# Scan decays in PSUM and 32-channel scan units in a decoder layer kernel (state space block, cross attention, ternary feed-forward)

## Chip, cores and metric

The kernel runs on one core of one Trainium2 chip. The metric is the device time of one execution in microseconds (us), the median of several runs. The engines are named as in the profile: PE is TensorE (matmuls; PEld its weight loads), DVE is VectorE, ACT is ScalarE, POOL is GpSimd, SP is SyncE, which issues all the DMAs of this kernel.

## What is computed

A batch of 16 sequences, 256 positions of width 512, goes through three blocks, each followed by x = layernorm(x + block(x)), all in float32.

```python
# 1. state space block: 1024 channels d, 16 states n, 256 steps l
hs, gate = x @ W_in_states.T, x @ W_in_gates.T
hs = silu(conv4(hs) + conv_b)                       # causal, along l
dt = softplus((hs @ W_dt.T) @ W_dtproj.T + b_dtproj)
Bm, Cm = hs @ W_b.T, hs @ W_c.T                     # 16 states each
dA  = exp(-exp(A_log) * dt)                         # decay, [d, n, l]
dBu = dt * Bm * hs                                  # input, [d, n, l]
h_l = dA_l * h_{l-1} + dBu_l                        # the scan along l
y = sum_n(h * Cm) + D * hs
out = (y * silu(gate)) @ W_out.T
# 2. cross attention: 16 heads of 16, 512 x 512 scores a head,
#    softmax(mask * q.k / 4 - (1 - mask) * 1e6) * mask, times v
# 3. feed-forward: activations rounded to 8 bits, ternary weights,
#    silu(a) * b, rounded again, down projection
```

## The kernel before

The function decoder_kernel writes the work of each batch as short pieces (Python functions) in named streams: G and P are the projections (prep), R the step widths dt and the rows B and C, M the scan, T and U the output projection, K, L, A and N the attention, F the feed-forward. The table WIN gives each stream a stretch of time, counted in batches from the start of its batch's scan; place spreads the pieces over it, and the pieces of all batches are emitted in the order of these times. So the scan of one batch, the attention of the one before and the feed-forward of the one before that run side by side. The framework's scheduler then fixes the order of instructions on each engine; each engine works its list in order.

**Scan (lines 351 to 403).** Channels are on partitions, 128 in each of eight tiles d. A unit is one tile d and four of the 16 states, 4 x 256 columns. POOL makes the scan's input (line 382, B times dt*u); ACT makes the decay with four exponentials, one a state, with a different scale each (line 392), into one of two SBUF buffers dA; VectorE scans 1024 columns in one instruction (line 394), where a zero first decay of each state stops the carry from the state before. Three units later (LAG) POOL multiplies by C (line 362), in six of eight units VectorE adds the upper two states to the lower two (line 369), and PE adds up the states by matmuls with an identity into the PSUM tile red (line 371). At the end of a tile d VectorE adds D*u (line 374). B and C are DMA-broadcast to all 128 partitions.

```python
t = dA_t[dA_i[0] % DAB]
for j in range(4):
    n = q * 4 + j
    nc.scalar.activation(t[:, j, 1:], st["dt"][d // 4][:, d % 4, 1:], AF.Exp, scale=A[:, d, n : n + 1])
nc.vector.tensor_tensor_scan(seg, t.rearrange("p n l -> p (n l)"), seg, 0.0, ALU.mult, ALU.add)
```

**Projections (240 to 348).** inproj makes u with three convolution steps on VectorE (line 280), a tanh and a product of two SBUF tensors (line 287). gate computes silu(gate) early (lines 253 to 264), stores it in DRAM (sgd), and gated (line 466) loads it back when the scan is done. softplus works on SBUF tiles of 1024 columns (lines 333 to 348), and dtu is formed in the scan (line 379).

**Attention (406 to 593).** split_store (line 434) writes q and k to DRAM in a part of reduced precision and a remainder (line 440). step(i) computes the scores of a head twice: once for the row maxima (lines 505 and 535), and once transposed, where ACT takes the exponentials (line 540), which are multiplied by the values with 32 columns of weights (line 546). Each of four heads has its own quarter of PE's columns (tile_position); the product of a head comes after that head's exponentials.

**PSUM.** Its eight banks are shared out by BANK (line 40): two for projections, output and feed-forward (mm), four for scores and attention projections (sc), one for the values' sums (av), one for the states' sums (red). The norm (line 223) and the feed-forward's scale factors (lines 600 to 613) mix tiny VectorE steps with one POOL power (line 231).

Of the kernel before, what the change touches and what calls it, by code (L numbers as in the profile page):

```python
# [36 lines left out]
WIN = {'G': (-1.4, -1.15), 'P': (-1.15, -0.888), 'R': (-0.611, -0.455), 'M': (0.0, 0.8), 'T': (0.476, 0.576), 'U': (0.812, 0.912), 'L': (0.991, 1.041), 'K': (0.773, 0.826), 'A': (1.018, 1.938), 'N': (2.099, 2.147), 'F': (2.57, 3.237), 'W': (0.0, 1.0)}  # L37
DAB = 2
UB = 4
BANK = {k: ("mm", 2) for k in "PGOFDW"} | {k: ("sc", 4) for k in "VXKQS"} | {"Y": ("av", 1), "E": ("red", 1)}  # L40
VW = HD + 1
HB = 5
PTB = 5
QKB = 10
SPT, SPN = "h", HB
F4B = 3
ONPOOL = "n"
LAG = 3
SGB = 1
S2OFF = 2  # L50
TREE_V = (0,1,3,4,5,7)
# [3 lines left out]
def decoder_kernel(ctx, tc, x, xT, ctx_in, mask, winT, wdtT, wbcT, wdpT, woutT, dvec, wqkvT, bqk, bv, wguT, wdnT, out):  # L55
# [15 lines left out]
    def eng(k):  # L71
        return nc.gpsimd if k in ONPOOL else nc.vector

# [32 lines left out]
    # A = -exp(A_log); conv weights and D, W_c carry the halves of the tanh forms  # L106
    A = const([P, NDT, NS], F32, "A")
    nc.scalar.activation(A, dv[:, :, 7:23], AF.Exp)
    nc.vector.tensor_scalar(A, A, -1.0, None, ALU.mult)
# [8 lines left out]

    dA_t = []
    for i in range(DAB):  # L120
        t = const([P, 4, L], F32, f"dA{i}")
        nc.vector.memset(t[:, :, 0:1], 0.0)
        dA_t.append(t)
    dA_i = [0]

# [5 lines left out]
    # Score operands in DRAM, 64 rows a head: rows 2..49 three slots of split q or k, 50..55 split  # L131
    # mask terms, 0, 1, 62, 63 ones in k and zeros in q (the maxima take their place on chip).
# [90 lines left out]
    def layernorm(r, o):  # L223
        st = at("lst", [P, 2, 6], 2)
        mv = at("lmv", [P, 2, 2], 2)
        for i in range(2):
            nc.vector.bn_stats(st[:, i, :], r[:, i, :])
            nc.vector.bn_aggr(mv[:, i, :], st[:, i, :])
        rs = at("lrs", [P, 2], 2)
        nc.vector.tensor_scalar(rs, mv[:, :, 1], LN_EPS, None, ALU.add)  # L230
        nc.gpsimd.tensor_tensor(rs, rs, mhalf, ALU.pow)  # L231
        nb = at("lnb", [P, 2], 2)
        nc.vector.scalar_tensor_tensor(nb, mv[:, :, 0], -1.0, rs, ALU.mult, ALU.mult)
        for i in range(2):
            nc.scalar.activation(o[:, i, :], r[:, i, :], AF.Identity, bias=nb[:, i : i + 1], scale=rs[:, i : i + 1])
# [4 lines left out]
    def prep(b):  # L240
# [3 lines left out]
        def load():  # L244
            st["xT"] = []
            for k in range(4):
                t = mt("xT", [P, L], 4)
                nc.sync.dma_start(out=t, in_=xT[b, k * P : (k + 1) * P, :])
                st["xT"].append(t)
            st["u"] = [None, None]  # L250
            st["sgd"] = dr.tile([P, NDT, L], F32, tag="sgd", name=nm("sgd"), bufs=3)

        def gate(d0):
            g = mm_ps([P, 2, L], "G")
            for i in range(2):
                d = d0 + i
                w = mt("win", [P, 4, P], 3)
                nc.sync.dma_start(out=w, in_=winT[:, :, DI + d * P : DI + (d + 1) * P])
                for k in range(4):
                    nc.tensor.matmul(g[:, i, :], w[:, k, :], st["xT"][k], start=k == 0, stop=k == 3)  # L260
            sg = mt("sg", [P, 2, L], SGB)
            nc.scalar.activation(sg, g, AF.Tanh, scale=0.5)
            nc.vector.scalar_tensor_tensor(sg, sg, 1.0, g, ALU.add, ALU.mult)  # L263
            nc.sync.dma_start(out=st["sgd"][:, d0 : d0 + 2, :], in_=sg)

        def inproj(d0):
            hs = mm_ps([P, 2, L], "P")
            z = mt("tmp", [P, 2, L], 2)
            for i in range(2):
                d = d0 + i  # L270
                w = mt("win", [P, 4, P], 3)
                nc.sync.dma_start(out=w, in_=winT[:, :, d * P : (d + 1) * P])
                for k in range(4):
                    nc.tensor.matmul(hs[:, i, :], w[:, k, :], st["xT"][k], start=k == 0, stop=k == 3)  # L274
# [11 lines left out]
            nc.scalar.activation(u, z, AF.Tanh)  # L286
            eng("z").scalar_tensor_tensor(u, u, 1.0, z, ALU.add, ALU.mult)  # L287
# [20 lines left out]
        def bcast():  # L308
            st["B"], st["C"] = [], []
            for half in range(2):  # L310
                for nmk, o in (("B", 0), ("C", NS)):
                    t = mt(nmk, [P, 8, L], 2)
                    src = st["bcd"][o + half * 8 : o + half * 8 + 8, :]
                    nc.sync.dma_start(out=t, in_=src[None].broadcast_to([P, 8, L]))
                    st[nmk].append(t)

        def dtpre():
            st["dt"] = []
            for hf in range(2):
                X = mt("dt", [P, 4, L], 3)  # L320
                st["dt"].append(X)
# [9 lines left out]

        def softplus():
            xs = [X.rearrange("p a l -> p (a l)") for X in st["dt"]]
            es = []
            for X in xs:
                e = mt(SPT, [P, 4 * L], SPN)
# [3 lines left out]
            for X, e in zip(xs, es):  # L340
                W = mt(SPT, [P, 4 * L], SPN)
                nc.vector.tensor_scalar(W, e, 1.0, -1.0, ALU.add, ALU.add)
                eng("r").scalar_tensor_tensor(X, X, 0.0, W, ALU.max, ALU.subtract)
                eng("x").tensor_tensor(X, X, e, ALU.add)
            for e in es:
                nc.scalar.activation(e, e, AF.Ln, bias=1.0)
            for X, e in zip(xs, es):
                nc.vector.tensor_tensor(X, X, e, ALU.add)  # L348

        g = [load] + [lambda d=d: gate(d) for d in range(0, NDT, 2)]  # L350
        th = [lambda d=d: inproj(d) for d in range(0, NDT, 2)]
        return {"G": g, "P": th, "R": [ts_bc, bcast, dtpre, softplus]}

# [1 line left out]
    def scan(b):  # L355
        st = S[b]
        th = []
        pend = []

        def tail(job):  # L360
            d, q, hh = job
            nc.gpsimd.tensor_tensor(hh, hh, st["C"][q // 2][:, 4 * (q % 2) : 4 * (q % 2) + 4, :], ALU.mult)  # L362
            if q == 0:
                st["red"] = mm_ps([P, 512], "E")
            red = st["red"]
            m = 4
            if (4 * d + q) % 8 in TREE_V:
                m = 2
                nc.vector.tensor_tensor(hh[:, 0:2, :], hh[:, 0:2, :], hh[:, 2:4, :], ALU.add)  # L369
            for n in range(m):  # L370
                nc.tensor.matmul(red[:, :L], ident, hh[:, n, :], start=q + n == 0, stop=q == 3 and n == m - 1)  # L371
            if q == 3:
                u = st["u"][d // 4][:, d % 4, :]
                nc.vector.scalar_tensor_tensor(u, u, dv[:, d, 5:6], red[:, :L], ALU.mult, ALU.add)

        def unit(d, q):
            if q == 0:
                dtu = mt("dtu", [P, L], 2)
                nc.vector.tensor_tensor(dtu, st["dt"][d // 4][:, d % 4, :], st["u"][d // 4][:, d % 4, :], ALU.mult)  # L379
                st["dtu"] = dtu  # L380
            hh = mt("h", [P, 4, L], HB)
            nc.gpsimd.tensor_tensor(  # L382
                hh,
                st["B"][q // 2][:, 4 * (q % 2) : 4 * (q % 2) + 4, :],
                st["dtu"][:, None, :].broadcast_to([P, 4, L]),
                ALU.mult,
            )
            t = dA_t[dA_i[0] % DAB]
            dA_i[0] += 1
            for j in range(4):  # L390
                n = q * 4 + j
                nc.scalar.activation(t[:, j, 1:], st["dt"][d // 4][:, d % 4, 1:], AF.Exp, scale=A[:, d, n : n + 1])  # L392
            seg = hh.rearrange("p n l -> p (n l)")
            nc.vector.tensor_tensor_scan(seg, t.rearrange("p n l -> p (n l)"), seg, 0.0, ALU.mult, ALU.add)  # L394
            pend.append((d, q, hh))
# [3 lines left out]
        for d in range(NDT):  # L399
            for q in range(4):  # L400
                th.append(lambda d=d, q=q: unit(d, q))
# [4 lines left out]
    def attn(b):  # L406
# [4 lines left out]
        def load():  # L411
# [14 lines left out]
            st["so"] = dr.tile([4, P, H], F32, tag="so", name=nm("so"), bufs=2)  # L426
# [348 lines left out]
```

## Time and profile before

| | |
|---|---|
| three runs | 5077.5, 5086.9, 5097.3 us; median 5086.9 us |
| profiled execution, span from first to last instruction | 5091.4 us |
| granted PE clock, mean | 0.874 of full |
| DMA | 592.7 MB on the main queue, 37.1% of 16 engines' time |
| ACT exponentials of the decay (line 392) | 2048 x 496 ns |
| row maxima (line 535) | 1024 x 678 ns |
| ACT waits for the scan before it fills dA | 1127.2 us, 403 times |

In a row of instructions the profile gives the line, the engine, the operation, out<-in by tile name, the shape and the count; then after the bar the busy time in us, the mean duration in ns, and the engine's idle time just before these instructions with what ended it. A row of one tile's instructions gives shortest, median and longest duration in ns. The chain of work that ended last runs for 50% of its time over DVE and for 29% over PE.

### The profile page before, as it was taken

To read this page: it belongs to the slowest core of one execution; us is meant where nothing else is said; L and a number is where in the kernel's file an instruction comes from. 1 tells how busy PE (TensorE), PEld (TensorE's weight loads), DVE (VectorE), ACT (ScalarE), POOL (GpSimd) and SP (SyncE) were. 2 spreads that over 40 slices of the span, in tenths; PEclk is the share of its full clock that TensorE was granted. 3 is DMA by queue.
4 is the path that set the end of the run, shared out by engine and by line. 5 is a ranking of instruction groups with operands and counts; after the bars stand their busy time and mean duration, and the time that the engine had idled before them with its cause. 6 is when DMAs were issued, how large, how long until landed. Compare 5 with 4: busy or idle time off the path is not lost.

```text
span 5091.4 us, 41958 instructions
## 1 busy us (share of the span) xinstructions
PE 4207.6 (83%) x12802; PEld 1966.2 (39%) x12802; DVE 4421.5 (87%) x4282; ACT 2284.0 (45%) x4506; POOL 3229.4 (63%) x1143
## 2 busy tenths in 40 slices
PE   6456877988889898888888899897888889887986
PEld 4333343444433444444344344343444334333332
DVE  4999899989999898999989897997979899898542
ACT  3243434444445444444544444454454444443433
POOL 2747767858678485767757584685849577477100
PEclk8677888988889898889989889898999989897988
DMA  7362232343432434344243433424343243333332
GB/s 210 106 216 88 77 115 81 119 125 115 124 129 80 134 113 132 120 121 134 88 143 100 130 115 114 135 85 130 112 140 114 78 151 97 116 106 96 96 109 79
DMA packets 416618, 595.42 MB, mean 117 GB/s; under 512 B 47416, under 2 KB 203064, under 8 KB 408200
## 3 DMA queue, kind: packets, MB, share of 16 engines
q1 hardware_dynamic: 416392, 592.74, 37.1%
q8 instruction: 101, 1.65, 0.1%
q14 instruction: 125, 1.02, 0.1%
HBM read 493.39 MB, written 105.51 MB: 118 GB/s over the span
## 4 chain that ended last, share of the span: by engine, by line
DVE 50%; PE 29%; issue 7%; DMA 5%; ACT 2%; POOL 1%; SPq 1%; DVEq 0%; ACTq 0%; POOLq 0%
DVE h L394 19%; PE av L546 8%; DVE h L369 7%; DVE mx L535 6%; PE sc L505 6%; PE red L371 4%; DVE dtu L379 2%; PE mm L481 2%; DVE tmp L280 2%; PE mm L260 1%; PE mm L677 1%; PE mm L274 1%; DVE u L287 1%; DVE qf L440 1%; DVE dt L348 1%
## 5 line engine op out<-in xcount | busy, mean ns | idle before, releaser
L382 POOL TENSOR_TENSOR h<-B,dtu 128x1024 f32<-128x1024 f32 x512 | 1622.3, 3178 | 511.7 <-PE red L371 182.3
L362 POOL TENSOR_TENSOR h<-h,C 128x1024 f32<-128x1024 f32 x512 | 1480.0, 2896 | 652.3 <-DVE h L394 607.2
L394 DVE TENSOR_TENSOR_SCAN h<-dA,h 128x1024 f32<-128x1024 f32 x512 | 1614.5, 3157 | 2.3 <-POOL h L382 2.2
L392 ACT ACTIVATE dA<-dt,A 128x255 f32<-128x255 f32 x2048 | 877.3, 496 | 1192.3 <-DVE h L394 1127.2
L546 PE MATMUL av<-pT,vaug 128*32 128x512 f32 x2048 | 1039.0, 646 | 10.8 <-ACT pT L540 10.3
L371 PE MATMUL red<-h,ident 128*128 128x256 f32 x2560 | 770.6, 439 | 318.9 <-DVE h L369 271.3
L505 PE MATMUL sc<-qk,qk 64*128 64x512 f32 x2048 | 865.1, 518 | 195.6 <-DVE mx L535 103.9
L535 DVE TENSOR_REDUCE mx<-sc 128x1 f32<-128x512 f32 x1024 | 672.4, 678 | 264.2 <-PE sc L505 262.6
L540 ACT ACTIVATE pT<-sc 128x512 f32<-128x512 f32 x1024 | 581.7, 588 | 474.5 <-PE sc L505 472.9
L505 PEld LDWEIGHTS sc<-qk,qk 64*128 64x128 f32 x2048 | 351.1, 203 | 1101.7 <-issue 670.0
L371 PEld LDWEIGHTS red<-h,ident 128*128 128x128 f32 x2560 | 520.8, 215 | 557.6 <-DVE h L369 334.4
L369 DVE TENSOR_TENSOR h<-h 128x512 f32<-128x512 f32 x384 | 663.8, 1730 | 1.6 <-POOL h L362 1.6
L481 PE MATMUL mm<-wout,u 128*128 128x512 f32 x512 | 297.8, 692 | 40.1 <-DMA wout<-in_woutT 17.6
L581 POOL TENSOR_TENSOR qk<-qk,qk 128x512 f32<-128x512 f32 x32 | 47.9, 1498 | 443.9 <-DMA qk<-sr 340.7
L274 PE MATMUL mm<-xT,win 128*128 128x256 f32 x1024 | 273.7, 417 | 37.9 <-DMA win<-in_winT 21.3
L260 PE MATMUL mm<-xT,win 128*128 128x256 f32 x1024 | 264.7, 412 | 44.1 <-DMA win<-in_winT 20.9
L546 PEld LDWEIGHTS av<-pT,vaug 128*32 128x32 f32 x2048 | 132.3, 111 | 324.3 <-issue 223.1
L260 PEld LDWEIGHTS mm<-xT,win 128*128 128x128 f32 x1024 | 204.3, 206 | 120.1 <-DVE f L639 32.7
L274 PEld LDWEIGHTS mm<-xT,win 128*128 128x128 f32 x1024 | 205.0, 207 | 105.4 <-issue 28.7
L280 DVE SCALAR_TENSOR_TENSOR tmp<-mm,cw,tmp 128x254 f32<-128x254 f32 (+2 forms) x384 | 180.0, 471 | 36.9 <-ACT tmp L277 33.4
L231 POOL TENSOR_TENSOR lrs<-lrs,mhalf 128x2 f32<-128x2 f32 x48 | 53.4, 1118 | 246.4 <-DVE lrs L230 237.3
L642 PE MATMUL mm<-fw,xqT 128*128 128x512 fp8e4 x512 | 153.9, 429 | 38.5 <-DVE sg L263 18.4
(116 smaller groups left out, 3927.7 us busy)
## 6 DMA issues: line engine op xcount, KB each, us to landing
win<-in_winT SPq DMA_DIRECT2D x256, 256.0 KB
wout<-in_woutT SPq DMA_DIRECT2D x256, 256.0 KB
fw<-gu_q SPq DMA_DIRECT2D x256, 256.0 KB
B<-bcd SPq DMA_DIRECT2D x32, 1024.0 KB
C<-bcd SPq DMA_DIRECT2D x32, 1024.0 KB
qk<-sq SPq DMA_DIRECT2D x128, 256.0 KB
qk<-sk SPq DMA_DIRECT2D x128, 256.0 KB
fw<-dn_q SPq DMA_DIRECT2D x128, 256.0 KB
```

The source lines that it names most:

```text
L260: nc.tensor.matmul(g[:, i, :], w[:, k, :], st["xT"][k], start=k == 0, stop=k == 3)
L274: nc.tensor.matmul(hs[:, i, :], w[:, k, :], st["xT"][k], start=k == 0, stop=k == 3)
L362: nc.gpsimd.tensor_tensor(hh, hh, st["C"][q // 2][:, 4 * (q % 2) : 4 * (q % 2) + 4, :], ALU.mult)
L369: nc.vector.tensor_tensor(hh[:, 0:2, :], hh[:, 0:2, :], hh[:, 2:4, :], ALU.add)
L371: nc.tensor.matmul(red[:, :L], ident, hh[:, n, :], start=q + n == 0, stop=q == 3 and n == m - 1)
L382: nc.gpsimd.tensor_tensor(hh, st["B"][q // 2][:, 4 * (q % 2) : 4 * (q % 2) + 4, :], st["dtu"][:, None, :].broadcast_to([P, 4, L]), ALU.mult,)
L392: nc.scalar.activation(t[:, j, 1:], st["dt"][d // 4][:, d % 4, 1:], AF.Exp, scale=A[:, d, n : n + 1])
L394: nc.vector.tensor_tensor_scan(seg, t.rearrange("p n l -> p (n l)"), seg, 0.0, ALU.mult, ALU.add)
L505: nc.tensor.matmul(p, lhs[rows, c * P : (c + 1) * P].bitcast(F32R), rhs[rows, :].bitcast(F32R), start=True, stop=True)
L535: nc.vector.tensor_reduce(st[("mx", i // G)][:, i % G, k : k + 1], p, AX.X, ALU.max)
L540: nc.scalar.activation(e, p, AF.Exp, scale=DSC)
L546: nc.tensor.matmul(av[32 * k : 32 * k + 32, :], vaug_f[:, i2 % 4, c0 : c0 + 32], pT[k], start=i2 % 4 == 0, stop=i2 % 4 == 3, tile_position ...
```

## The change

It touches many places at once. A scan unit becomes 32 channels and all 16 states: four groups of states on the partitions (4 x 32), four states and 256 steps on the columns. For this dt and dt*u go through DRAM (dtd) and are loaded replicated (dtr, dur), and B and C are loaded once per group of states. The decay is written to two PSUM banks, two states each, and each unit has two scans of 512 columns. The adds of line 369 are gone; the states' sums of four units are taken together by matmuls with 32 columns of weights (sel) in four column groups. The values' products also come in four groups of 256 columns, all after the exponentials of two heads. The gate is projected where it is used and not stored. VectorE steps that had two SBUF operands take one of them from PSUM (u, softplus, q/k remainder, gate). Tiny steps of norm and feed-forward go to POOL. PSUM: two banks mm (projections, output, states' sums), three sc (scores, attention projections, feed-forward), two dA, one av. The h buffers grow from five to eight; pT becomes three buffers of two heads.

```diff
-BANK = {k: ("mm", 2) for k in "PGOFDW"} | {k: ("sc", 4) for k in "VXKQS"} | {"Y": ("av", 1), "E": ("red", 1)}
+BANK = {k: ("mm", 2) for k in "PGOE"} | {k: ("sc", 3) for k in "VXKQSFDW"}
-HB = 5
-PTB = 5
+NB4 = 4
+DB = P // NB4
+HB = 8
+PTB = 3
-LAG = 3
+LAG = 2
...
+    sel = const([P, DB], F32, "sel")
+    nc.vector.tensor_reduce(sel, ident.rearrange("p (n d) -> p d n", n=NB4), AX.X, ALU.add)
...
-    for i in range(DAB):
-        t = const([P, 4, L], F32, f"dA{i}")
+    for i in range(2):
+        t = ps.tile([P, 2, L], F32, tag=f"dA{i}", name=f"dA{i}", bufs=1)
...
-        nc.vector.tensor_scalar(rs, mv[:, :, 1], LN_EPS, None, ALU.add)
+        nc.gpsimd.tensor_scalar(rs, mv[:, :, 1], LN_EPS, None, ALU.add)
         nc.gpsimd.tensor_tensor(rs, rs, mhalf, ALU.pow)
-        nc.vector.scalar_tensor_tensor(nb, mv[:, :, 0], -1.0, rs, ALU.mult, ALU.mult)
+        nc.gpsimd.tensor_tensor(nb, mv[:, :, 0], rs, ALU.mult)
+        nc.gpsimd.tensor_scalar(nb, nb, -1.0, None, ALU.mult)
...
-            nc.scalar.activation(u, z, AF.Tanh)
-            eng("z").scalar_tensor_tensor(u, u, 1.0, z, ALU.add, ALU.mult)
+            nc.scalar.activation(hs, z, AF.Tanh)
+            nc.vector.scalar_tensor_tensor(u, hs, 1.0, z, ALU.add, ALU.mult)
...
+                    t = mm_ps([P, 2, L], "P")
+                    nc.scalar.activation(t, e, AF.Identity, bias=1.0)
+                    nc.vector.scalar_tensor_tensor(t, t, 1.0, e, ALU.subtract, ALU.subtract)
+                    nc.vector.scalar_tensor_tensor(t, X, 0.0, t, ALU.max, ALU.subtract)
+                    nc.vector.tensor_tensor(t, t, l, ALU.add)
+                    dtu = mt("dtu", [P, 2, L], 2)
+                    nc.vector.tensor_tensor(dtu, t, st["u"][hf][:, s, :], ALU.mult)
+                    nc.scalar.copy(X, t)
+                    for k, src in ((0, X), (1, dtu)):
+                        for i in range(2):
+                            dst = st["dtd"][k, 4 * hf + 2 * i2 + i].rearrange("c g l -> g c l")
+                            nc.sync.dma_start(out=dst, in_=src[:, i, :])
...
+        def fetch(d):
+            st["rep"] = []
+            for k, tag in ((0, "dtr"), (1, "dur")):
+                t = mt(tag, [P, NB4, L], 2)
+                src = st["dtd"][k, d].rearrange("c g l -> c (g l)")
+                nc.sync.dma_start(out=t, in_=src[None].broadcast_to([NB4, DB, NB4 * L]))
+                st["rep"].append(t)
 
         def tail(job):
-            d, q, hh = job
-            nc.gpsimd.tensor_tensor(hh, hh, st["C"][q // 2][:, 4 * (q % 2) : 4 * (q % 2) + 4, :], ALU.mult)
...
-                nc.vector.tensor_tensor(hh[:, 0:2, :], hh[:, 0:2, :], hh[:, 2:4, :], ALU.add)
-            for n in range(m):
-                nc.tensor.matmul(red[:, :L], ident, hh[:, n, :], start=q + n == 0, stop=q == 3 and n == m - 1)
+            d, hh = job
+            done.append((hh, nc.gpsimd.tensor_tensor(hh, hh, st["C"], ALU.mult)))
+            if len(done) < NB4:
+                return
+            red = mm_ps([P, 512], "E")
+            for j in range(NS // NB4):
+                for g, (h, _) in enumerate(done):
+                    m = nc.tensor.matmul(
+                        red[DB * g : DB * g + DB, :L], sel, h[:, j, :], start=j == 0, stop=j == NS // NB4 - 1, tile_position=(0, DB * g)
+                    )
+                    if j == 0 and g < NB4 - 1:
+                        after(m, done[-1][1], True)
...
+            nc.gpsimd.tensor_tensor(hh, st["B"], dtu[:, g, None, :].broadcast_to([P, NS // NB4, L]), ALU.mult)
+            for h2 in range(2):
+                t = dA_t[dA_i[0] % 2]
+                dA_i[0] += 1
+                for i in range(2):
+                    j = 2 * h2 + i
+                    nc.scalar.activation(t[:, i, 1:], dt[:, g, 1:], AF.Exp, scale=A[:, d, g, j : j + 1])
+                seg = hh[:, 2 * h2 : 2 * h2 + 2, :].rearrange("p n l -> p (n l)")
+                nc.vector.tensor_tensor_scan(seg, t.rearrange("p n l -> p (n l)"), seg, 0.0, ALU.mult, ALU.add)
...
-            f = qf([P, H])
-            nc.vector.scalar_tensor_tensor(f, p, bqk_t[:, m, bcol : bcol + 1], st["mb"], ALU.add, ALU.mult)
+            nc.vector.scalar_tensor_tensor(p, p, bqk_t[:, m, bcol : bcol + 1], st["mb"], ALU.add, ALU.mult)
...
-            sg = mt("sgl", [P, 4, L], 1)
-            nc.sync.dma_start(out=sg, in_=st["sgd"][:, 4 * hf : 4 * hf + 4, :])
...
+        def gated(d0):
+            g = mm_ps([P, 2, L], "G")
+            project(g, st["xTg"], DI + d0 * P)
+            t = mt("tmp", [P, 2, L], 2)
+            nc.scalar.activation(t, g, AF.Tanh, scale=0.5)
+            nc.vector.scalar_tensor_tensor(g, t, 1.0, g, ALU.add, ALU.mult)
+            u = st["u"][d0 // 4][:, d0 % 4 : d0 % 4 + 2, :]
+            nc.vector.scalar_tensor_tensor(u, u, 0.5, g, ALU.mult, ALU.mult)
...
+                for t in range(2):
+                    for j in range(G):
+                        k = 2 * t + j
+                        c0 = (G * g + j) * VW
+                        m = nc.tensor.matmul(
+                            av[32 * k : 32 * k + 32, :],
+                            vaug_f[:, c, c0 : c0 + 32],
+                            e[:, j, t * L : (t + 1) * L],
...
+                        if j < G - 1:
+                            after(m, x, True)
```

## The prediction, made before the changed kernel ran

> **What bounds the kernel now.** I read the page first, then the durations of single tiles' instructions, the busy time by stretch, and PE's timeline.
>
> ```profile
> PE 4207.6 (83%) x12802; PEld 1966.2 (39%) x12802; DVE 4421.5 (87%) x4282; ACT 2284.0 (45%) x4506; POOL 3229.4 (63%) x1143
> ...
> L382 POOL TENSOR_TENSOR h<-B,dtu 128x1024 f32<-128x1024 f32 x512 | 1622.3, 3178 | 511.7 <-PE red L371 182.3
> L362 POOL TENSOR_TENSOR h<-h,C 128x1024 f32<-128x1024 f32 x512 | 1480.0, 2896 | 652.3 <-DVE h L394 607.2
> L394 DVE TENSOR_TENSOR_SCAN h<-dA,h 128x1024 f32<-128x1024 f32 x512 | 1614.5, 3157 | 2.3 <-POOL h L382 2.2
> ...
> L546 PE MATMUL av<-pT,vaug 128*32 128x512 f32 x2048 | 1039.0, 646 | 10.8 <-ACT pT L540 10.3
> L371 PE MATMUL red<-h,ident 128*128 128x256 f32 x2560 | 770.6, 439 | 318.9 <-DVE h L369 271.3
> ...
> L369 DVE TENSOR_TENSOR h<-h 128x512 f32<-128x512 f32 x384 | 663.8, 1730 | 1.6 <-POOL h L362 1.6
> ```
>
> VectorE and TensorE are both nearly full, so a change must relieve both. The same instruction's shortest, middle and longest duration (ns) shows that VectorE's fullness is partly waiting. From the instructions on tile h, then from line 643:
>
> ```profile
> L382 POOL TENSOR_TENSOR h<-B,dtu x512: 2332/2803/5524, 91.0 to 4725.3; 128x1024 f32<-128x1024 f32 x171
> L394 DVE TENSOR_TENSOR_SCAN h<-dA,h x512: 2246/3126/4459, 93.5 to 4737.1; 128x1024 f32<-128x1024 f32 x171
> ...
> L369 DVE TENSOR_TENSOR h<-h x384: 651/1742/2869, 105.0 to 4748.2; 128x512 f32<-128x512 f32 x192
> ```
> ```profile
> L643 DVE TENSOR_TENSOR f<-f,mm x128: 648/673/690, 867.6 to 5069.6; 128x512 f32<-128x512 f32 x128
> ```
>
> Lines 394 and 369 read two SBUF tensors and stretch by up to one POOL instruction; L643, one operand in PSUM, never does. Third, the stretches: from first to last scan unit, then the end.
>
> ```profile
> 91.00:4760.00 4669.00, 3883.79 (x11779) 1833.16 (x11779) 4265.29 (x3979) 2131.31 (x4256) 3213.55 (x1122) 0.87 0.37 116
> 4760.00:5091.40 331.40, 268.07 (x824) 92.21 (x823) 128.13 (x251) 127.23 (x209) 14.20 (x14) 0.88 0.33 99
> ```
>
> (Columns: busy PE, PEld, DVE, ACT, POOL, granted clock, DMA.) Head 91, middle 4669 (DVE 91%, PE 83%), end 331 us. Last, PE's timeline:
>
> ```profile
> 2401.13 1.05 PE L546 MATMUL av<-pT,vaug 128*32 128x512 f32 x2
> 2402.11 0.49 PE L505 MATMUL sc<-qk,qk 64*128 64x512 f32 x1
> ...
> 2403.59 1.05 PE L546 MATMUL av<-pT,vaug 128*32 128x512 f32 x4
> 2404.57 1.99 PE L371 MATMUL red<-h,ident 128*128 128x256 f32 x8
> ```
>
> One value product alone (two f32 parts) and two neighbours in different column groups both take 0.98 us to the next start. Groups do run together, but only when nothing stands between them.
>
> **The change, part by part.** The profiled span is 5091.4 us, 0.1% over the median 5086.9; I sum against the span.
>
> *VectorE.* Leaves, by rows: scans 1614.5, half adds L369 663.8, dtu L379 184.1, softplus L342/343/344/348 204.5, L287 95.1, L440 88.0, L470 77.3, tiny steps sent to POOL (L230, 233, 653, 604, 607, 610, 612) 131.8; together 3059.1 in 1504 instructions. Comes: 1024 scans of 512; four steps for each of 64 softplus blocks, and 3x64 steps for u, the q/k remainder and the second gate product. Undisturbed plain steps take 1206 for 1024 elements (L192) and 676 for 512 (L154), so 146 ns are fixed; of the undisturbed 1024 scan's 2246, 2100 halve to 1050, and a 512 scan is about 1196: 1225 us, 73 more than 512 x 2246, the price of halving it. The 448 other steps at 0.68 (L643, L154): 304. Together 1529 in 1472 instructions. The counts nearly agree, so the 80 ns or so by which neighbours overlap in the records cancel: 4421.5 - 3059 + 1529 = 2890 us; nearly all of it is in the middle: 4265 - 1530 = 2735.
>
> No row shows a scan with a PSUM operand. [...]
>
> *TensorE.* L546: 512 sets of four products, 256 columns each. In the order of the changed program 511 sets stand unbroken. A set costs 0.98 less half its streaming 0.43 = 0.55, times 1.04 (mean 1039.0/1024 against 0.98): 0.57 x 512 = 292 instead of 1039. L371 gives way to 2048 products with 32 columns, 16 a block in four groups: four rounds of two parts at 0.24 = 2.0, x128 x1.04 = 265. The order breaks these blocks into 257 runs: 129 breaks at about 0.5 us (two part-filled rounds) add 65: 330 against 770.6. In the middle (939 of av there, 30 in the end after): 3884 - 939 - 771 + 262 + 330 = 2770 us. Gate products only move: same 1024 projection products, same 64 pairs of loads; sgd's 64 stores and 32 loads vanish.
>
> With L369 gone PE no longer waits for it (271 and 334 us of matmuls and weight loads); next late is POOL's product with C, since a block of sums waits for four of them. Their tiles are held until then: up to seven of the eight h buffers, so a late block stops POOL's next product after about one unit (6 us). Today PE's sums hold POOL for 182 us; I leave that in the shares below.
>
> *POOL.* 1024 products at 2.34 undisturbed 2400, lines 581/582 at 1.25 80, L231 at 0.70 34, 224 new tiny steps at 0.1 to 0.7 (a one-element memset to L231), taken 0.3: 67. Total 2580 instead of 3229. The four-step norm now sits in POOL's queue, but takes no turn behind VectorE in between.
>
> *ACT.* 2048 exponentials stay, now into PSUM; no row shows that. Bounds -50 to +100 ns each (rows from PSUM are cheaper: L622 468 with bias, against L392's 496); taken 0, since 496 is the nearest row. 64 more Identity and 64 copies at 0.6 to 0.68, 64 more av copies: +90: 2374.
>
> *DMA and SP.* Out: sgd/sgl 33.6 MB, B/C 67.1. In: dtr/dur 256 x 512 KB = 134.2, dtd 256 x 128 KB = 33.6, B/C 16.8, a second xT 8.4: 593 becomes 685 MB. At today's 1889 us of all engines for 593, 2180. SP issues 2628 rows instead of 2296. Each dtr/dur load waits on SP for ACT or POOL to free a buffer, and queued behind it stand weights for PE and score operands. With two buffers a load is due a whole group (four units, some 25 us) ahead, longer than most of SP's waits today; I cost it at 0. If that cover fails, 128 group starts lose a landing of 3 to 5 us: 400 to 600.
>
> *Ends.* In the last stretch av's 100 us become 30, and PE is 81% busy there: 331 - 60 = 270. The head loses the gate work but gains dtd's round trip and 16 small loads for A, which stand ahead of the first exponentials (89.5 us today): 90.
>
> **Sum.** The middle now holds PE 2770, DVE 2735, POOL some 2570, ACT 2220. If PE kept its 83%: 3340 + 360 = 3700. But four engines are now close, exponentials run through two half-size PSUM buffers, and scores, feed-forward and projections of attention share three banks instead of four and two. No row prices this; I take two points, 81%: 2770/0.81 = 3420, and 3420 + 90 + 270 = **3780 us**. At 88%: 3510; at 72%: 4210.
>
> **The rivals.**
> - *Coupling eats more* (0.20). Three shared banks, or SP's waits, hold PE near 73%: 3795 + 360 = 4150. For it: ACT waits 1127 us for scans today, PE loads wait 210 for VectorE to free scores. [...]
> - *Column groups of the sums do not overlap* (0.07): the change does not do what it says. 2048 products alone at 0.5: 1070 instead of 330, PE 3510 at 85% + 360: 4490. Against: the x4 row.
> [...]
> - *Scan and exponential in turn* (0.04), the slow side. A buffer's two exponentials start only after its scan. If ACT, in order, has two score exponentials (0.59) ahead of them, VectorE idles 2x0.49 + 2x0.59 + 0.2 = 2.4 us a half scan: 2735 + 1024x2.4 + 360 = 5550. It ends slower from 1.95 us, (5091 - 360 - 2735)/1024. For it: 399 of 1023 neighbouring scans stand directly behind each other. Against: today's idle before scans is 2.3 us in all, and 624 have other work between.
>
> **Numbers.** Likeliest 0.62 at 3780 (own range 3600 to 3980). The range 3490 to 4250 leaves out the two worst rivals, part of the smooth one and the edge of the coupled. A measurement tells about 0.5% from no change: the turn-taking case is the slower 0.04, its milder half-way ends and the worst of the unoverlapped sums give same 0.01, the rest is faster, 0.95.
>
> **What would show it.** Right: scans near 1.18 us with longest close to shortest, POOL products near 2.35 with little spread, DVE near 2890, PE near 3050 with av 290 and sums 330. Wrong: stretched scans, PE well over 3400, idle before scans in hundreds of us, or waits for dtr, dur or sc on top.

## The result, and the profile after

The changed kernel takes 5127.3 us in the median (5120.8 to 5132.9, four runs) against 5088.3 us before: ratio 1.0074, 95% interval 1.0049 to 1.0099. It is slower by 0.7%, small but outside the noise, where 3780 us and a clear gain were forecast. The profiled execution's span is 5121.4 us, the granted clock 0.751 (before 0.874).

The page of the changed kernel:

```profile
PE 3462.3 (68%) x16386; PEld 1616.7 (32%) x16386; DVE 2966.0 (58%) x4254; ACT 2421.9 (47%) x4700; POOL 2544.8 (50%) x1367
...
q1 hardware_dynamic: 488456, 685.29, 43.4%
...
PE 31%; DMA 27%; DVE 18%; ACT 9%; SPq 4%; issue 4%; POOL 1%; DVEq 0%; ACTq 0%; POOLq 0%
...
L403 POOL TENSOR_TENSOR h<-B,dur 128x1024 f32<-128x1024 f32 x512 | 1196.2, 2364 | 1272.4 <-PE mm L389 858.1
...
L409 ACT ACTIVATE dA<-dtr,A 128x255 f32<-128x255 f32 x2048 | 951.5, 473 | 855.7 <-DVE h L411 775.6
...
L411 DVE TENSOR_TENSOR_SCAN h<-dA,h 128x512 f32<-128x512 f32 x1024 | 1210.4, 1207 | 58.7 <-ACT dA L409 42.8
...
L506 PE MATMUL mm<-wout,u 128*128 128x512 f32 x512 | 329.3, 752 | 418.2 <-DMA wout<-in_woutT 392.6
...
L574 PE MATMUL av<-pT,vaug 128*32 128x256 f32 x4096 | 436.4, 495 | 49.6 <-ACT pT L564 47.4
L389 PE MATMUL mm<-h,sel 128*32 128x256 f32 x4096 | 397.3, 472 | 94.6 <-POOL h L383 86.7
```

The work did shrink: VectorE 4421 to 2966 us, POOL 3229 to 2545, TensorE 4208 to 3462. But no engine is over 68% busy, and the span is no shorter: all of them but ScalarE (45% to 47% busy) stand idle more. The chain of work that ended last tells where: transfers hold 27% of it, 5% before. The waits say the same (us in total, times, longest); the last line is the kernel before, for the same weights:

```profile
POOL h L403 <- PE mm L389: 858.1, 67, 35.8
...
ACT pT L564 <- PE sc L530: 768.8, 330, 28.7
...
DVE mx L558 <- PE sc L530: 539.2, 289, 12.0
...
PE mm L506 <- DMA wout<-in_woutT: 392.6, 56, 24.5
```
```profile
PE mm L481 <- DMA wout<-in_woutT: 17.6, 20, 2.8
```

One such place, by windows (columns as before: PE, PEld, DVE, ACT, POOL, clock, DMA share, GB/s), and in the timeline of SP and PE:

```profile
2040.00:2050.00 10.00, 5.83 (x33) 2.21 (x31) 6.06 (x8) 7.62 (x18) 5.92 (x3) 1.00 0.30 116
2050.00:2060.00 10.00, 0.00 (x0) 0.00 (x0) 0.00 (x0) 0.00 (x0) 0.00 (x0) 0.67 0.42 137
2060.00:2073.00 13.00, 0.16 (x1) 0.16 (x1) 0.00 (x0) 0.00 (x0) 0.00 (x0) 0.50 0.50 142
```
```profile
2053.57 0.88 SPq L378 DMA_DIRECT2D dur<-dtd  x1
2054.55 1.54 SPq L264 DMA_DIRECT2D win<-in_winT  x1
2056.18 1.24 SPq L378 DMA_DIRECT2D dtr<-dtd  x1
2057.51 4.41 SPq L93 DMA_DIRECT2D wout<-in_woutT  x2
...
2072.84 2.07 PE L506 MATMUL mm<-wout,u 128*128 128x512 f32 x2 [24.50 <-DMA wout<-in_woutT]
```

For 23 us the whole core stands still. PE has waited for its weights since 2048.3; SP issues the tile at 2057.5, after slow issues of its own (the two for wout take 4.41 us, where one takes 0.36 in the median), and PE goes on at 2072.8, some 15 us after the issue. Yet the DMA share is only 0.42 to 0.50: half of the DMA engines' time is free while the compute engines wait for a transfer. That is the contradiction to explain.

**Four engines.** The trace has every packet's start and duration. In the changed kernel packets of 4096 bytes (38,912, of 191 ns; the loads of dtr, dur, B and C send 36,864 of them) move exactly four at a time in 70% of the time in which any of them moves, and more than five at a time in under 2% of it. Before, the same size moved sixteen at a time more often than any other number (15% of its time), and more than five at a time in 73%. The new loads and stores have 4 as their slowest dimension: a load reads [4, 32, 1024] with the 4 a broadcast, a store writes [4, 32, 256]. The packets of 1024 bytes (79,744 of 54.5 ns, 32,768 of them from the stores of dtd) move exactly four at a time in 32% of their time, before in 8%. The reading here is that a transfer with 4 as its slowest dimension runs on four of the sixteen engines, the same four each time: two such loads, issued at 2033.1 us (dtr) and 2033.7 (dur), move four packets at a time for 11 us, not eight. The trace does not tell which four.

What that means for one of the four, worked out: dtr and dur 32,768 packets x 191 ns / 4 = 1566 us; B and C 4096 x 191 / 4 = 196; dtd 32,768 x 54.5 / 4 = 446; and a sixteenth of all else (43.4% of 16 x 5121 us less the above: 26,720 us) 1670. Together an estimated 3880 of 5121 us, 76%, against 1670 us, 33%, on the other twelve. The profile's 43.4% is the mean of these. What that does to a transfer over all sixteen is in the packets of the stall. The three wout tiles that SP issues from 2057.5 to 2062.4 have 384 packets of 2048 bytes. 288 of them, twelve sixteenths, start from 2062 to 2066. Then none starts for 4 us, while packets of 4096 bytes (256 from 2058 to 2072: one dtr and one dur) go on four at a time. The last 96, four sixteenths, start from 2070.4 to 2073.7, and PE goes on at 2072.8. By this reading the tiles waited for their shares on the four busy engines while the other twelve had long finished theirs.

### The profile page after: what moved, and what is told of

The parts are those of the page before. It is cut to its first block, busy times and chain, and to the rows that moved or that the text cites. A ratio compares the mean times of both kernels' runs of the same rounds, so it can differ in the third digit from the quotient of the medians.

```text
span 5121.4 us, 50817 instructions
## 1 busy us (share of the span) xinstructions
PE 3462.3 (68%) x16386; PEld 1616.7 (32%) x16386; DVE 2966.0 (58%) x4254; ACT 2421.9 (47%) x4700; POOL 2544.8 (50%) x1367
## 3 DMA queue, kind: packets, MB, share of 16 engines
q1 hardware_dynamic: 488456, 685.29, 43.4%
## 4 chain that ended last, share of the span: by engine, by line
PE 31%; DMA 27%; DVE 18%; ACT 9%; SPq 4%; issue 4%; POOL 1%; DVEq 0%; ACTq 0%; POOLq 0%
DVE h L411 9%; DMA wout<-in_woutT 8%; PE mm L266 6%; PE sc L530 6%; PE mm L389 4%; DVE mx L558 4%; PE mm L506 4%; DMA md<-mhl 3%; PE av L574 3%; DMA sq<-qf 3%; ACT pT L564 2%; DMA qk<-sk 2%; PE sc L718 2%; DMA fw<-dn_q 2%; ACT dA L409 2%
## 5 line engine op out<-in xcount | busy, mean ns | idle before, releaser
L403 POOL TENSOR_TENSOR h<-B,dur 128x1024 f32<-128x1024 f32 x512 | 1196.2, 2364 | 1272.4 <-PE mm L389 858.1
L383 POOL TENSOR_TENSOR h<-h,C 128x1024 f32<-128x1024 f32 x512 | 1199.3, 2363 | 371.0 <-DVE h L411 327.5
L409 ACT ACTIVATE dA<-dtr,A 128x255 f32<-128x255 f32 x2048 | 951.5, 473 | 855.7 <-DVE h L411 775.6
L411 DVE TENSOR_TENSOR_SCAN h<-dA,h 128x512 f32<-128x512 f32 x1024 | 1210.4, 1207 | 58.7 <-ACT dA L409 42.8
L574 PE MATMUL av<-pT,vaug 128*32 128x256 f32 x4096 | 436.4, 495 | 49.6 <-ACT pT L564 47.4
L389 PE MATMUL mm<-h,sel 128*32 128x256 f32 x4096 | 397.3, 472 | 94.6 <-POOL h L383 86.7
L286 DVE SCALAR_TENSOR_TENSOR tmp<-mm,cw,tmp 128x255 f32<-128x255 f32 (+2 forms) x384 | 182.7, 478 | 247.0 <-ACT tmp L283 240.7
L389 PEld LDWEIGHTS mm<-h,sel 128*32 128x32 f32 x4096 | 151.9, 131 | 306.5 <-issue 170.3
L718 PE MATMUL sc<-fw,f 128*128 128x512 fp8e4 x512 | 137.4, 415 | 140.9 <-DMA fw<-dn_q 140.6
L678 PE MATMUL sc<-fw,xqT 128*128 128x512 fp8e4 x512 | 164.9, 454 | 23.3 <-DVE mx L558 13.4
```

Of the source, the lines that this page charges most:

```text
L383: done.append((hh, nc.gpsimd.tensor_tensor(hh, hh, st["C"], ALU.mult)))
L389: m = nc.tensor.matmul(red[DB * g : DB * g + DB, :L], sel, h[:, j, :], start=j == 0, stop=j == NS // NB4 - 1, tile_position=(0, DB * g))
L403: nc.gpsimd.tensor_tensor(hh, st["B"], dtu[:, g, None, :].broadcast_to([P, NS // NB4, L]), ALU.mult)
L409: nc.scalar.activation(t[:, i, 1:], dt[:, g, 1:], AF.Exp, scale=A[:, d, g, j : j + 1])
L574: m = nc.tensor.matmul(av[32 * k : 32 * k + 32, :], vaug_f[:, c, c0 : c0 + 32], e[:, j, t * L : (t + 1) * L], start=c == 0, stop=c == 3, t ...
L718: nc.tensor.matmul(p, hT[:, 4 * q + i, :], w[:, i, :], start=q + i == 0, stop=q == 3 and i == 3)
```

## The experiments

Theory A: transfers confined to four engines hold up all others. Rivals: B, SP's in-order queue and its number of issues; C, the PSUM banks as regrouped (scores, feed-forward and attention projections in three instead of four and two); D, the lower clock as cause. Any edit also makes the framework's scheduler lay out the lists anew, so every difference between two runs has a new order of instructions in it too (VectorE's list in e_ctl4 has the instruction of e_all16 in 55% of its places). In most variants lines are shifted by two (L411 of the changed kernel is L413).

**Transfers spread over sixteen engines (e_all16).**

```diff
-st["dtd"] = dr.tile([2, NDT, DB, NB4, L], ...)
+st["dtd"] = dr.tile([2, NDT, NB4, DB, L], ...)
-nc.sync.dma_start(out=t, in_=src[None].broadcast_to([NB4, DB, NB4 * L]))
+for n in range(NB4):
+    nc.sync.dma_start(out=t[n * DB : (n + 1) * DB], in_=src)     # src [32, 4, 256]
...
-dst = st["dtd"][k, ...].rearrange("c g l -> g c l")
+dst = st["dtd"][k, ...].rearrange("g c l -> (g c) l")
```

> The changed kernel with its scan transfers spread: the DRAM copy of dt and dt*u laid out group by group so that one store writes 128 rows, and each load of a group (and of B and C) issued as four loads of 32 partitions. Same bytes; about 860 more transfers issued on SP. Theory A (transfers whose slowest dimension is 4 run on four of the 16 DMA engines, and those four are the bound): the small packets then run about 16 wide, the waits for wout, qk and the replicated tiles mostly go, and the time falls to 3900 to 4400 us. Theory B (SP's in-order queue and its number of issues is the bound): with more issues it is not faster, 5100 to 5500. Theory C (three shared PSUM banks and two half-size decay buffers): unchanged within 3%, 5000 to 5250. Theory D (the lower granted clock is the cause): unchanged, clock near 0.75.

Measured: 4428.0 us, ratio 0.869 (0.866 to 0.872), clock 0.793. As theory A has it, just past its upper edge. From its page, and its waits:

```profile
PE 3358.0 (76%) x16386; PEld 1588.5 (36%) x16386; DVE 2967.5 (67%) x4254; ACT 2411.7 (54%) x4700; POOL 2545.4 (57%) x1367
...
q1 hardware_dynamic: 607112, 685.37, 55.1%
```
```profile
POOL h L405 <- PE mm L391: 508.1, 56, 27.9
ACT pT L566 <- PE sc L532: 498.0, 304, 9.4
...
PE mm L508 <- DMA wout<-in_woutT: 51.7, 35, 7.2
```

Same bytes, more packets, a higher DMA share, and the wait for wout falls from 393 to 52 us. VectorE, ACT and POOL do the same work to within 11 us: only idle time went. SP issues 864 transfers more, but its issuing takes 1797 us instead of 1938, and the longest issue of wout 1.7 us instead of 4.8.

**The control (e_ctl4).** The same number of transfers in the same layout, each over all 128 partitions of one quarter of the tile, so that its slowest dimension is 4 again:

```diff
-for n in range(NB4):
-    nc.sync.dma_start(out=t[n * DB : (n + 1) * DB], in_=src)
+for g in range(NB4):
+    nc.sync.dma_start(out=t[:, g, :], in_=src[g][None].broadcast_to([NB4, DB, L]))
```

> The same kernel as the first, same number of transfers, same bytes and same 1 KB runs, but each of the four loads of a group covers all 128 partitions of one quarter of the tile, so that its slowest dimension is 4 again. Only the replicated loads differ. Theory A: the loads' 1900 us per engine stay on four engines; the stores and B, C have left them, so 4700 to 5150 us, clearly above the first. Theory B, C, D: the same as the first within 2%.

Measured: 4770.2 us, ratio 0.938 (0.936 to 0.940), in theory A's range. Its wait for wout:

```profile
PE mm L508 <- DMA wout<-in_woutT: 140.1, 41, 9.3
```

Its 1 KB packets (loads and stores have that size now) move exactly four at a time in 45% of their time, in e_all16 in 5%. SP's issues, as many as in e_all16 (3905), take 2250 us instead of 1797. In the program only the spreading of the replicated loads differs between the two, and the time differs by 342 us; B is out as the main cause. The rest of the gain (5127 to 4770) comes with the stores, B and C, and with the new order.

**Loads alone (e_load16).** Each load split by partitions as in e_all16, layout and stores unchanged.

> Only the replicated loads of dt and dt*u split in four loads of 32 partitions with their 4 KB runs; layout, stores, B and C as in the changed kernel. Theory A: the four engines lose some 1400 us of 4150 and are no bound any more: 3950 to 4500 us. Theory B: 768 more issues on SP, 5100 to 5500. C and D: within 3% of 5127.

Measured: 4596.9 us, ratio 0.904 (0.902 to 0.905), a little over A's range: the loads alone give 530 of the 699 us.

**Loads issued from ScalarE (e_actq).**

```diff
-nc.sync.dma_start(out=t, in_=src[None].broadcast_to([NB4, DB, NB4 * L]))
+nc.scalar.dma_start(out=t, in_=src[None].broadcast_to([NB4, DB, NB4 * L]))
```

> The changed kernel with only the replicated loads (256 transfers) issued from ScalarE instead of SP; where they run and their bytes are as before. Theory B (a load that waits for its buffer on SP holds up all loads behind it): SP is freed, 4300 to 4800 us. Theory A: the four engines still have all of it, 5000 to 5400. C, D: within 3% of 5127.

Measured: 5095.3 us, ratio 1.0021 (1.0010 to 1.0032). Taking 256 loads out of SP's queue gives 0.6%. The 4096-byte packets still move at most five at a time in 98% of their time, and PE still waits for wout:

```profile
PE mm L506 <- DMA wout<-in_woutT: 277.3, 53, 15.8
```

**No replicated loads to speak of (x_noload).** On top of e_all16. (In fact 14 of a batch's 16 loads are left out, 117.4 MB and 896 issues, not the 15 and 126 of the expectation.)

> On top of the version with spread transfers (4428 us), 15 of each batch's 16 replicated loads of dt and dt*u are left out: one pair is loaded per batch and its later groups work on it again, so their values are those of the first group. 126 MB and 960 of SP's issues go. Theory A (spreading over 16 engines removed the transfer bound): little is left to gain, 4250 to 4400. If the transfers, or SP's issues, still bound the spread version: 3700 to 4100, with PE's clock going to 0.85 or over.

Measured: 4311.2 us, ratio 0.847 (0.845 to 0.850). Once spread, the replicated loads cost some 117 us, a new order included; what else holds the kernel at 4300 is not these loads.

**Decays back in SBUF (x_dasb).**

```diff
-t = ps.tile([P, 2, L], F32, tag=f"dA{i}", name=f"dA{i}", bufs=1)
+t = const([P, 2, L], F32, f"dA{i}")
-QKB = 10
+QKB = 8
```

> The version with spread transfers (4428 us), with the two decay buffers back in SBUF, still half size; 8 qk buffers instead of 10 make the room. PSUM banks stay as they are. If the PSUM operand is what keeps POOL and VectorE from stretching each other: scans go from 1.21 to 1.4 to 1.7 us in the mean, POOL's products from 2.36 to 2.9, exponentials from 473 to about 496 ns, 4600 to 5000 us. If it isn't: 4400 to 4500 and scans stay at 1.21.

Measured: 5314.4 us, ratio 1.044 (1.041 to 1.047), worse than either case of the expectation. Its groups (busy, mean ns, then idle before and its releaser), then the scan's shortest, median and longest duration in it and in the changed kernel:

```profile
L413 DVE TENSOR_TENSOR_SCAN h<-dA,h 128x512 f32<-128x512 f32 x1024 | 2269.7, 2245 | 13.6 <-POOL h L405 10.8
L405 POOL TENSOR_TENSOR h<-B,dur 128x1024 f32<-128x1024 f32 x512 | 1423.9, 2806 | 909.0 <-PE mm L391 561.8
L385 POOL TENSOR_TENSOR h<-h,C 128x1024 f32<-128x1024 f32 x512 | 1393.3, 2728 | 676.5 <-DVE h L413 635.3
L411 ACT ACTIVATE dA<-dtr,A 128x255 f32<-128x255 f32 x2048 | 926.6, 500 | 1512.4 <-DVE h L413 1479.4
```
```profile
L413 DVE TENSOR_TENSOR_SCAN h<-dA,h x1024: 1154/2292/3429, 102.0 to 4979.3; 128x512 f32<-128x512 f32 x171
```
```profile
L411 DVE TENSOR_TENSOR_SCAN h<-dA,h x1024: 1154/1210/1225, 110.5 to 4771.8; 128x512 f32<-128x512 f32 x171
```

The scan of 512 columns goes from 1207 to 2245 ns in the mean, POOL's products from 2363 and 2365 to 2806 and 2728. So it is the PSUM operand that keeps the two engines apart, as the prediction's L643 (648 to 690 ns) hinted; the shortest scan is 1154 ns with either source. It matters more with half-size scans: one of 512 loses in the mean about as much here (2245 less 1207: 1040 ns) as one of 1024 lost before (3157 less the shortest, 2246: 910), and there are twice as many.

**The banks.** Five runs change only the BANK line, four of them on top of e_all16: the feed-forward's sums back in mm (x_ffnmm; the output projection's, which the expectation names too, had never left mm); sc 2 and mm 3 (y_sc2); mm 1 for the state sums alone and sc 4 for all else (z_e1sc4); all five in one pool (z_pool5). The fifth has the one pool on the changed kernel itself, transfers left as they were (w_pool5only).

```diff
-BANK = {k: ("mm", 2) for k in "PGOE"} | {k: ("sc", 3) for k in "VXKQSFDW"}
+BANK = {k: ("sc", 5) for k in "PGOEVXKQSFDW"}
```

> The version with spread transfers (4428 us), with the feed-forward and output-projection sums of attention put back from the three shared sc banks to the two mm banks, as before the change. Theory C (scores wait for banks that the feed-forward holds): TensorE's and ScalarE's waits for sc shrink, 4150 to 4350. If the shared banks cost nothing: 4400 to 4600, as mm's two banks then serve projections, sums and feed-forward.

Measured: 4435.2 us, ratio 0.871 (0.869 to 0.873): nothing gained.

> Spread transfers (4428 us) with one PSUM bank taken from sc (2 instead of 3) and given to mm (3 instead of 2). If the three shared banks are a large part of what keeps it above the forecast (theory C): 4700 to 5100, with longer waits for sc. If they are not: 4380 to 4550.

Measured: 4944.4 us, ratio 0.973 (0.971 to 0.976); 516 us lost with one bank of sc. Its largest wait for sc (498 in e_all16):

```profile
ACT pT L566 <- PE sc L532: 808.6, 468, 9.6
```

> Spread transfers (4428 us), with one mm bank for the state sums alone and four sc banks for all else, projections of the state space block included. Theory C: 4000 to 4300. If the state sums in one bank then wait for VectorE's step on them and hold the h tiles: 4400 to 4600.

Measured: 4407.7 us, ratio 0.867 (0.863 to 0.870): nothing to speak of gained. POOL's wait for the state sums falls (508 to 233 us), but it now waits 562 us for a softplus step of ScalarE (line 345).

> Spread transfers (4428 us), with the two mm and three sc banks made one pool of five for all uses. If banks that stand in the wrong group hold the scores (theory C): 4000 to 4250, with shorter waits for sc. If the banks' number and not their grouping counts: 4350 to 4550.

Measured: 4164.5 us, ratio 0.819 (0.817 to 0.820), the fastest of all runs. From its page (busy time and one group), then from its waits:

```profile
PE 3080.6 (74%) x16386; PEld 1546.6 (37%) x16386; DVE 2927.1 (70%) x4254; ACT 2414.2 (58%) x4700; POOL 2551.1 (61%) x1367
...
L532 PE MATMUL sc<-qk,qk 64*128 64x512 f32 x2048 | 687.8, 551 | 464.9 <-DVE mx L560 160.3
```
```profile
ACT pT L566 <- PE sc L532: 305.7, 308, 4.6
...
DVE mx L560 <- PE sc L532: 194.4, 109, 7.8
...
POOL h L405 <- PE sc L391: 97.2, 26, 34.2
```

The waits for scores fall from 498 and 422 to 306 and 194 us, POOL's wait for the state sums from 508 to 97. Score products also lie beside each other more: the same 2048 keep PE busy 688 us instead of 903. How much of it is banks, and how much the new order, these runs don't separate: VectorE's list agrees with that of e_all16 in 26% of its places, though in 32% in x_ffnmm too, which gained nothing.

> The changed kernel (5127 us) with one pool of five PSUM banks; its transfers stay as they are, dt and dt*u on four DMA engines. Theory A (the four engines set the pace): the pool gains little, 4980 to 5130. Theory C (banks as strong on their own): 4800 to 4900, as much as the pool gave with spread transfers (264 us) or more.

Measured: 4814.3 us, ratio 0.946 (0.943 to 0.949). Theory A's number for this run fails, C's holds: the pool gives 313 us even with the transfers on four engines. But the wait for wout stays:

```profile
PE sc L506 <- DMA wout<-in_woutT: 399.7, 49, 20.9
```

So two causes lie side by side and nearly add up:

| us | banks 2 + 3 | one pool of 5 |
|---|---|---|
| four-engine transfers | 5127 | 4814 |
| spread transfers | 4428 | 4164 |

**The h tiles and other steps.** The first run is on top of e_all16, the next ones on top of what their expectation names:

> The version with spread transfers (4428 us) with nine h buffers instead of eight and eight qk buffers instead of ten. POOL waits 508 us there for the state sums to free an h tile. If that wait sets the pace: 4250 to 4380 us, the wait falls under 350. If it is only where a lead shows up: 4400 to 4480.

Measured: 4351.2 us, ratio 0.854 (0.851 to 0.857), the wait at 473: a gain of 77 us, yet the named wait hardly moved.

> The best version so far (4351 us) with POOL's product with C one unit behind the scan instead of two, so that the h tiles come free one unit earlier. If h tiles set POOL's pace: 4220 to 4320, the wait for state sums (473 us) falls under 350. If POOL then waits for the scan instead: 4350 to 4500.

Measured: 4317.7 us, ratio 0.849 (0.847 to 0.851); the wait is 386 us, and POOL waits as long, 386, for the scan: both cases in part.

> Spread transfers with ten h and six qk buffers. If another h tile is worth what the ninth was (77 us): 4270 to 4320. If the score operands with six buffers cost it again: 4350 to 4500.

Measured: 4435.2 us, ratio 0.873 (0.871 to 0.875): the gain of the ninth is gone. PE waits for qk loads 69 times (191 us) instead of 16 (99), which fits six qk buffers being too few; the two were not changed apart.

> The best version so far (spread transfers, nine h and eight qk buffers, 4351 us) with the changed kernel's DRAM layout kept: stores split into four of 32 partitions, loads into four of 32 partitions with 4 KB runs instead of 1 KB. Fewer, larger packets, 768 more issues on SP. If packet time still counts: 4230 to 4320. If SP's issuing counts: 4400 to 4500. If neither bounds it: 4320 to 4390.

Measured: 4526.0 us, ratio 0.890 (0.889 to 0.892): 175 us worse than with 1 KB runs. Packet size was not worth it; whether the additional issues or the other order cost it stays open.

With one pool the same steps gain nothing (14 and 23 us slower), and with one mm bank they lose 134 us.

> The best version so far (nine h and eight qk buffers, product with C one unit behind the scan, 4318 us) with one pool of five banks. If it adds up with what the pool alone gains or loses: 4318 plus that difference, within 50 us.

> The best version so far (4318 us) with one mm bank for the state sums and four sc banks for the rest. If it adds up with what the split alone gains or loses: 4318 plus that difference, within 50 us.

> Spread transfers and one pool of five banks (4164 us), with POOL's product with C one unit behind the scan, eight h and ten qk buffers. If the two qk buffers taken away cost the combined version its gain: 4090 to 4150. If the earlier product itself costs it in the pool: 4165 to 4220.

Measured: z_pool5b 4187.6 us, ratio 0.823 (0.822 to 0.825), where 4054 would be the sum; z_e1sc4b 4541.2, ratio 0.894 (0.891 to 0.898), where 4297 would be; w_pool5lag1 4178.9, ratio 0.821 (0.819 to 0.823), its second case. None adds up with the single steps. With the pool the likely reason, not tested, is that POOL's wait for the state sums, which these steps were to shorten, is mostly gone already (508 to 97 us).

## Why the prediction was wrong, step by step

- **VectorE, POOL, ACT: right.** 2966, 2545 and 2422 us against 2890, 2580 and 2374. That a scan with a PSUM operand is neither stretched by POOL nor dearer for its source, no row of before shows; in the 2890 and in POOL's 2580 it was the author's estimate. The runs showed it: a scan took 1207 ns against 1196 forecast, its longest 1225, its shortest 1154 with either source, and POOL's products took 2364 and 2363 ns; with the decays in SBUF (x_dasb) they took 2245, 2806 and 2728. The exponential into PSUM is cheaper: 473 ns, against 496 before and 500 in x_dasb. (The price of halving the scans comes to 75 us, not 73.)
- **DMA and SP: the step that failed.** The prediction set "At today's 1889 us of all engines for 593, 2180" and found room, and "I cost it at 0". As a mean, 2180 is right (43.4% of 5121 is 2223), but the new transfers don't use the mean: their packets move four at a time, on engines that are, by the estimate above, 76% busy. The bytes were counted and the access patterns not read. The issues were undercounted too: SP issued 3041 transfers instead of 2481, 560 more where the prediction has 332 (2628 for 2296); 192 of the others are the values' stores (so, 64 to 256). The fallback, "128 group starts lose a landing of 3 to 5 us: 400 to 600", looked at dtr and dur alone; the time was lost at whatever else, by that reading, came through the same four engines, wout first, with 15 us from issue to use in the place shown and stops of PE up to 24.5 us. Measured: spreading the transfers gave 699 us (650 with one pool), where the sum had 0.
- **Coupling: mis-sized, and the same error in kind as the rival "coupling eats more".** "Three shared banks, or SP's waits, hold PE near 73%" was given 0.20 and 4150 us. Between the first scan and about the last (102 to 4700 us) PE was busy 3104 of 4598 us, 68%: banks and transfers both came. The banks' part, new order included, is 264 to 313 us, and the two points allowed for it, 81% instead of 83%, would be some 80 us.
- **TensorE: work about right, time too low.** The parts of the forecast add up to some 3020, not 3050, from times at before's clock of 0.874. In time at full clock (busy time by mean clock, rough) 3050 is 2666; the changed kernel has 3462 x 0.751 = 2600, e_all16 3358 x 0.793 = 2663. A set of eight parts of av takes 570 ns to the next start where the clock is full, as forecast, and 1011 where it is half (206 of 460 sets). That is most of why av measured 436 us, not 292; the sums measured 397, not 330. The groups do overlap; that rival is out.
- **The clock (theory D)** follows. With transfers alone changed, it rose together with PE's busy share (all columns but the last two):

| | changed | e_ctl4 | e_load16 | e_all16 | x_noload | z_pool5 | before |
|---|---|---|---|---|---|---|---|
| PE busy | 68% | 72% | 74% | 76% | 77% | 74% | 83% |
| clock | 0.751 | 0.768 | 0.780 | 0.793 | 0.796 | 0.814 | 0.874 |

The mean share alone doesn't set it: z_pool5 has 0.814 at 74%. In the stall shown above PE stops at 2048.3 us, the clock is half from 2053.4 to 2077.3, 4.5 us longer than the stall, and a wout product then takes 1061 ns instead of 592. So the clock makes that stall dearer than its own length, but it is not what started it.
- **Ends: the head 20 us long, the end right only with one pool.** First scan at 110 us (90 forecast); 350 from the last scan's start in the changed kernel and in e_all16, 263 in z_pool5 (270 forecast).

Mended in this order, the 1347 us between 3780 and 5127 are thus 699 of transfers, 264 of banks (each with its new order), and 384 that are left at 4164. Of the 384 the head and the end hold some 5; the middle of z_pool5 has 2836 us of PE's work (2770 forecast) in 3804 us, 74.6% where 81% was taken. Of its 898 us before 1000 PE is busy in 64%, later (1000 to 3500) in 78%. What holds it there was not taken apart: the cause of these 384 us stays open.

## What to carry to other kernels

Read the access pattern of every new transfer before adding up its bytes: where the slowest dimension was 4, as in a broadcast to four copies, the packets moved four at a time (70% of their time), and a mean DMA share of 43% was, by estimate, four engines at three quarters. The sign in this trace was a core that waits for transfers while the DMA share is half, with packets of one size hardly ever (under 2% of their time) more than five at a time. And when a change frees the engines, look at what then holds back their work: here the PSUM banks, cut into two fixed groups, took another 264 to 313 us, which one common pool, with the order that the scheduler made for it, gave back. This kernel with both mended ran in 4164 us, 18% under the kernel before.

## What the runs showed that was not expected

- A scan with both operands in SBUF was stretched by nearly the same time whether it had 512 columns (2245 ns in x_dasb) or 1024 (3157 before), some 1040 and 910 ns in the mean. In these two kernels the loss went with the number of scans, so cutting the scan in two without moving its operand doubled it.
- Moving 256 loads from SP's queue to ScalarE's changed the time by 0.6%; spreading the same loads changed it by 10%.
- One bank fewer for the scores' group cost 516 us; one more in a fixed group gained 20; the same five banks in one pool gained 264.
